# A product of constants behind every third piece of the chains between two attentions

## The chip, the core and the metric

The kernel runs on one core of a Trainium2 chip. The metric is the device time of one execution in microseconds (us). Five engines work beside each other and wait for one another by semaphores: PE (TensorE, matrix products; its weight loads are listed apart as PEld), DVE (VectorE), ACT (ScalarE), POOL (GpSimd) and SP (SyncE, which here only issues DMAs). Each engine takes its own instructions strictly in the order in which the program lists them; the profile also lists the clock that PE was granted, as a share of its full speed.

## The reference, cut to what matters

A stack of eight sublayers works on `x` of 8 batches x 512 tokens x 128 features, all in float32. Each one is `x = x + layernorm(f(layernorm(x)))`:

```
x = x + ln(L0_attn(ln(x)))   # softmax attention, 16 heads of 8
x = x + ln(L0_ffn (ln(x)))   # shifted mix, sigmoid(r) * (relu(k)^2 @ W_v)
x = x + ln(L1_attn(ln(x)))   # test-time learning: one gradient step after each batch
x = x + ln(L1_ffn (ln(x)))   # 8 experts, each token to its best one, capacity 256 an expert
x = x + ln(L2_attn(ln(x)))   # linear attention, softplus of normalised q and k
x = x + ln(L2_ffn (ln(x)))   # 8 experts, each takes its 512 best tokens
x = x + ln(L3_attn(ln(x)))   # softmax attention with rotary positions
x = x + ln(L3_ffn (ln(x)))   # 4 experts, each token weighs up to four of them
```

Nothing of this is touched by the change.

## The kernel before, in words

The 512 tokens of a batch lie as four tiles of 128. Three stretches follow one another. In the first, `Attention.run` works through the scores of L0's attention and a `Background` pulls pieces of the following sublayers in between. In the last, the same class does L3's attention with L3's expert layer in the background. Between the two lies the stretch that the change is about. There the sublayers from L0's feed-forward to the router of L2's experts are written as Python generators, here called chains: a chain issues the instructions of one piece of its work and yields.

- `residuals` (L556) finishes L0's attention batch by batch, `Mix.chain` (L616) is L0's feed-forward, `Learn.chain` and `serve_chain` (L760, L919) are the learning layer, `Route.chain` (L971) is the router of L1's experts, with its scatters to HBM at L1060.
- `Passes.chain` (L1107) runs L1's experts, in two passes (after 5 and after 8 routed batches); one piece is one expert: its input's transposes (L1136), hidden products (L1148, 128x256) and output products (L1170).
- `Pairs.chain` (L1234) sets off one `Pairs.batch` (L1252) every five turns. Such a chain of some 28 pieces takes one batch through the gather of L1's results (L1265), L2's linear attention (projection L1304, key-value sums L1335, outputs L1351) and L2's gate (L1392). The gradual start makes several batches lie side by side in different pieces.

`Rounds.turn` (L1202) sets the order: it lets every living chain issue one piece, in the order of its list, and is called until no chain is left. So the program order on every engine is chain after chain, turn after turn. A normalisation inside the chains goes DVE (statistics, L203), POOL (root, L194), DVE (offset, L211), ACT (scaling, L217), then PE (`flip`, four transposes, L239) and ACT (copy out of PSUM, L240).

Everything that PE writes goes to PSUM, by way of `Ctx.bank` (L118). It hands out the eight banks of PSUM in turn, whoever asks; whoever gets a bank waits until the readers of the bank's last content, eight requests ago, have finished.

`self.ident` and `self.c` are constants that lie in SBUF from the start: the identity, and behind it a triangular matrix and others.

Of the kernel before, what the change touches and what calls it, by code (L numbers as in the profile page):

```python
# [17 lines left out]
P = 128  # L18
# [10 lines left out]
C_ID = 0  # L29
# [41 lines left out]
class Ctx:  # L71


    def __init__(self, es: ExitStack, tc: tile.TileContext, consts: bass.AP):
        self.tc = tc
        nc = self.nc = tc.nc
        pool = lambda name, bufs, **kw: es.enter_context(tc.tile_pool(name=name, bufs=bufs, **kw))
        self.keep = pool("keep", 1)
        self.shared = pool("shared", 2)
        self.dram = pool("dram", 1, space=DRAM)  # L80

        self.c = self.keep.tile([P, C_ALL], F32, name="consts_sb", tag="consts_sb")
        nc.sync.dma_start(self.c, consts)
        self.ident = self.c[:, C_ID : C_ID + P]
        self.triu = self.c[:, C_TRIU : C_TRIU + P]
        self.ones = self.keep.tile([P, P], F32, name="ones", tag="ones")
        nc.vector.memset(self.ones, 1.0)
        self.mhalf = self.keep.tile([P, 8], F32, name="mhalf", tag="mhalf")
        nc.vector.memset(self.mhalf, -0.5)
        self.x = [self.keep.tile([P, NJ, D], F32, name=f"x{b}", tag=f"x{b}") for b in range(B)]  # L90

        self.home = self.keep

        self.ps = pool("ps", 1, space=PSUM)
        self.turn = [0]
        es.enter_context(tc.manual_schedule())

        self.brisk = False
# [19 lines left out]
    def bank(self, name):  # L118
        self.turn[0] += 1
        return self.ps.tile([P, 512], F32, name=name, tag=f"bank{self.turn[0] % self.RING}", bufs=1)  # L120

    def work(self, shape, name, bufs=2, dtype=F32):
        return self.w.tile(shape, dtype, name=name, tag=name, bufs=bufs)
# [137 lines left out]
class Background:  # L261
# [29 lines left out]
    def turn(self, gen):  # L291

        self.first.remove(gen)
        self.first.append(gen)
        self.step(self.first, gen)
# [897 lines left out]
class Rounds:  # L1193


    def __init__(self, chains):
        self.chains = list(chains)

    def add(self, chain):
        self.chains.append(chain)  # L1200

    def turn(self):  # L1202
        for chain in list(self.chains):
            try:
                next(chain)
            except StopIteration:
                self.chains.remove(chain)


class Pairs:  # L1210
# [520 lines left out]
def l3_weights(cx: Ctx, Wqkv, bqkv, Wout, bout):  # L1731
    raws = [cx.fetched(w) for w in (Wqkv, Wout)]
    rows = cx.row(bqkv, "w3a_b"), cx.row(bout, "w3a_bo")
    yield
    yield cx.transposed(Wqkv, "w3a", raw=raws[0]), cx.transposed(Wout, "w3a_o", raw=raws[1]), *rows
# [214 lines left out]
@with_exitstack  # L1950
def kernel(ctx: ExitStack, tc: tile.TileContext, a: dict, out: bass.AP):
    cx = Ctx(ctx, tc, a["consts"])
    nc = tc.nc
    for b in range(B):
        nc.sync.dma_start(cx.x[b], a["L0_attn_x"][b].rearrange("(j p) d -> p j d", p=P))
    of = lambda layer, *names: [a[f"{layer}_{n}"] for n in names]
    route = Route(cx, *of("L1_ffn", "w_switch", "b_switch"))
    right = ExitStack()
    with cx.phase("first"):
        cx.w = right.enter_context(tc.tile_pool(name="chains", bufs=2, side="right"))  # L1960
        with cx.beside("attention") as ca:
            mix = Mix(cx, *of("L0_ffn", "W_r", "W_k", "W_v", "mu_r", "mu_k"))
            learn = Learn(cx, route, *of("L1_attn", "t_k", "t_v", "t_q", "W1", "b1", "W2", "b2"))
            chains = l0(cx, Attention(ca), *of("L0_attn", "Wq", "Wk", "Wv"), mix, learn)

        cx.brisk = True
        with cx.beside("between") as cb:
            rounds = Rounds(chains)
            passes = Passes(cb, route, *of("L1_ffn", "w1", "b1", "w2", "b2"))
            pairs = Pairs(cb, route, *of("L2_attn", "W_qkv"), *of("L2_ffn", "gate_w"))  # L1970
            rounds.add(passes.chain())
            rounds.add(pairs.chain(passes, mix, rounds))
            while route.done < B:
                rounds.turn()
            right.close()
            ce = right.enter_context(cx.beside("experts", side="right"))
            experts = Experts(ce, pairs, *of("L2_ffn", "ln_w", "ln_b", "fc1s", "b1s", "fc2s", "b2s"))
            while rounds.chains:
                rounds.turn()
    cx.brisk = False  # L1980
    with cx.phase("last"):
        at = Attention(cx)
        ffn = L3Ffn(cx, *of("L3_ffn", "W1", "b1", "W2", "b2", "Wu", "bu"), out)
        with cx.beside("staging") as cs:
            cs.home = cx.home
            weights = l3_weights(cs, *of("L3_attn", "Wqkv", "bqkv", "Wout", "bout"))
            ffn.load()
            weights = experts.run(cs, weights)
        right.close()
        cx.w = right.enter_context(tc.tile_pool(name="tiles", bufs=2, side="right"))  # L1990
        with right:
            l3(cx, at, experts, ffn, weights)
# [62 lines left out]
```

## Time and profile before

| | |
|---|---|
| median of 3 runs | 2139.75 us (2133.82 to 2141.98) |
| the profiled execution's own time | 2144.43 us |
| its span, first to last instruction | 2142.6 us |
| granted PE clock, mean over the span | 0.876 |
| busy shares of the span | PE 83%, PEld 48%, DVE 59%, ACT 51%, POOL 23% |
| PE instructions (matmul records) | 10918 |
| shares of the chain that ended last | PE 59%, DVE 23%, issue 5%, POOL 5%, ACT 4%, DMA 2% |

The chain that ended last is followed back from the last instruction: at each step to what released it, or to the instruction before it on its engine. "Issue" is time in which an engine waited for nothing that the profile shows. The page cuts the span into 40 slices of 53.6 us. A float32 product is two matmul records and two weight loads, a transpose is one of each. The stretch between the attentions, from the end of the first attention's last products to the last pieces of `Pairs.batch`, goes from about 735 to 1125 us of the span.

### The profile page before, as it was taken

What the parts mean: (1) busy time and instruction counts of PE and PEld (TensorE: products, weight loads), DVE (VectorE), ACT (ScalarE), POOL (GpSimd) and SP (SyncE); (2) the same over time, 40 slices, a digit from 0 to 9 for tenths busy, and PEclk for the clock granted to TensorE, in tenths of its full rate; (3) what the DMA queues carried; (4) which work ended last, traced back from release to release, by engine and by line L of the source; (5) the groups of instructions that cost most, each with busy time, mean ns of one, the idle gap of its engine ahead of it and who ended that gap; (6) DMA issues with size and microseconds to landing.
All of it is one profiled execution on the core that took longest, in us unless ns stands there. A gap on an engine that the chain in (4) does not pass through costs nothing.

```text
span 2142.6 us, 31783 instructions
## 1 busy us (share of the span) xinstructions
PE 1772.7 (83%) x10918; PEld 1019.4 (48%) x10918; DVE 1265.6 (59%) x3840; ACT 1084.8 (51%) x2272; POOL 502.9 (23%) x574
## 2 busy tenths in 40 slices
PE   3999899999989757467646773899999999999998
PEld 1444445454444446446336552444444445454566
DVE  2677776868676455446547322776666666566322
ACT  1566655656545433246651221366666565656553
POOL 1001110212111130453523484222122121110010
PEclk7899999899889868579565786799999999999999
DMA  5212101111010103134323132111101011000000
GB/s 126 36 36 37 31 20 29 27 32 38 15 26 11 54 21 96 44 92 113 87 75 99 25 43 34 32 31 29 28 7 32 9 31 29 12 7 11 1 11 11
DMA packets 197920, 81.84 MB, mean 38 GB/s; under 512 B 97460, under 2 KB 189530, under 8 KB 197760
## 3 DMA queue, kind: packets, MB, share of 16 engines
q1 hardware_dynamic: 190080, 73.61, 14.3%
q0 software_dynamic: 7680, 6.19, 1.9%
q8 instruction: 88, 1.44, 0.3%
q14 instruction: 72, 0.59, 0.1%
HBM read 45.25 MB, written 31.59 MB: 36 GB/s over the span
## 4 chain that ended last, share of the span: by engine, by line
PE 59%; DVE 23%; issue 5%; POOL 5%; ACT 4%; DMA 2%; SPq 1%; POOLq 0%; ACTq 0%; DVEq 0%
PE at_s L402 13%; PE at_o L420 11%; DVE at_mx L403 8%; PE at_st L409 7%; PE l3f_y_ps L1923 5%; PE l3f_h_ps L1916 5%; DVE ln_st L203 3%; PE flip L239 3%; POOL l2f_out L1679 2%; POOL l2f_xg L1074 1%; POOL ln_rs L194 1%; PE l2a_qkv_ps L1304 1%; PE l1f_h_ps L1148 1%; PE l1f_y_ps L1170 1%; PE at_ops L434 1%
## 5 line engine op out<-in xcount | busy, mean ns | idle before, releaser
L403 DVE TENSOR_REDUCE at_mx<-at_s 128x1 f32<-128x512 f32 x1024 | 639.5, 681 | 281.4 <-PE at_st L409 217.8
L412 ACT ACTIVATE at_e<-at_st 128x512 f32<-128x512 f32 x1024 | 533.8, 597 | 214.0 <-PE at_st L409 189.3
L402 PE MATMUL at_s<-qk 32*128 32x512 f32 x2048 | 585.7, 652 | 28.1 <-DMA qk<-qk_zero 21.1
L409 PE MATMUL at_st<-qk 32*128 32x512 f32 x2048 | 567.3, 656 | 9.4 <-ACT at_e L412 4.6
L402 PEld LDWEIGHTS at_s<-qk 32*128 32x128 f32 x2048 | 221.4, 194 | 179.2 <-issue 74.0
L194 POOL TENSOR_TENSOR ln_rs<-ln_ve,mhalf 128x4 f32<-128x4 f32 x136 | 138.6, 1019 | 700.9 <-DVE ln_ve L188 607.3
L409 PEld LDWEIGHTS at_st<-qk 32*128 32x128 f32 x2048 | 218.4, 191 | 107.0 <-issue 41.5
L420 PE MATMUL at_o<-at_e,pad_v 128*32 128x512 f32 x2048 | 246.8, 625 | 9.9 <-DVE at_mx L403 9.8
L420 PEld LDWEIGHTS at_o<-at_e,pad_v 128*32 128x32 f32 x2048 | 63.5, 114 | 190.2 <-issue 156.9
L1923 PEld LDWEIGHTS l3f_y_ps<-w3f,l3f_hT 128*128 128x128 f32 x1024 | 129.3, 193 | 41.9 <-issue 30.9
L1923 PE MATMUL l3f_y_ps<-w3f,l3f_hT 128*128 128x128 f32 x1024 | 133.0, 277 | 0.6 <-ACT l3f_hT L1917 0.5
L1916 PE MATMUL l3f_h_ps<-l3f_xT,w3f 128*128 128x512 f32 x256 | 130.8, 606 | 0.1
L1917 ACT ACTIVATE l3f_hT<-l3f_h_ps,w3f_b1c 128x512 f32<-128x512 f32 x128 | 87.3, 689 | 84.0 <-PE l3f_h_ps L1916 83.8
L428 ACT COPY at_ot<-at_o 128x512 f32<-128x512 f32 x64 | 37.5, 586 | 173.8 <-PE at_o L420 173.8
L1926 DVE SCALAR_TENSOR_TENSOR l3f_o<-l3f_y_ps,l3f_w,l3f_o 128x128 f32<-128x128 f32 x128 | 44.5, 349 | 117.7 <-PE l3f_y_ps L1923 117.4
L217 ACT ACTIVATE l_xn<-x,ln_off,ln_rs 128x128 f32<-128x128 f32 x96 | 39.4, 482 | 72.4 <-DVE ln_off L211 72.3
L239 PE MATMUL flip<-consts_sb,l_xn 128*128 128x128 f32 x96 | 30.8, 411 | 47.8 <-ACT l_xn L217 47.6
L375 POOL COPY pad_v<-l_in 128x128 f32<-128x128 f32 x32 | 9.4, 293 | 246.2 <-DMA l_in<-l_v 216.0
L203 DVE BATCH_NORM_STATS2 ln_st<-x 128x6 f32<-128x128 f32 x256 | 55.2, 278 | 9.6 <-POOL x L1366 3.3
L1766 POOL TENSOR_TENSOR l_qk<-l_r,consts_sb 128x256 f32<-128x256 f32 x32 | 22.0, 687 | 159.0 <-DVE l_r L1761 159.0
L434 PE MATMUL at_ops<-consts_sb,at_ot 128*128 128x128 f32 x256 | 42.2, 288 | 18.1 <-DVE at_mx L403 16.6
L1679 POOL DMA_INDIRECT l2f_out<-l2f_y,l2f_idx x32 | 50.7, 1585 | 25.4 <-DVE l2f_y L1676 16.6
(388 smaller groups left out, 2514.7 us busy)
## 6 DMA issues: line engine op xcount, KB each, us to landing
l1f_w<-in_L_ffn_w SPq DMA_DIRECT2D x32, 256.0 KB
l2f_parts<-l2f_out SPq DMA_DIRECT2D x32, 256.0 KB
l2f_out<-l1f_zero SPq DMA_DIRECT2D x24, 256.0 KB
l_qk<-l_qkT SPq DMA_DIRECT2D x16, 256.0 KB
qk<-l_qk SPq DMA_DIRECT2D x128, 32.0 KB
qk<-at_mt SPq DMA_DIRECT2D x256, 2.0 KB
qk<-l_qkT SPq DMA_DIRECT2D x128, 32.0 KB
l2f_x<-l2f_rows SPq DMA_DIRECT2D x8, 272.0 KB
```

Of the source, the lines that this page charges most:

```text
L194: self.nc.gpsimd.tensor_tensor(rs, ve, self.mhalf[:, :NJ], ALU.pow)
L203: nc.vector.bn_stats(st[:, j, :], src[:, j, :])
L239: self.nc.tensor.transpose(t[:, j * P : (j + 1) * P], src[:, j, :], self.ident)
L402: nc.tensor.matmul(s, qk[:, 0, c * P : (c + 1) * P], qk[:, 1, :], start=True, stop=True)
L403: nc.vector.tensor_reduce(mx[n][:, c, h : h + 1], s, AX.X, ALU.max, negate=True)
L409: nc.tensor.matmul(s, qk[:, 1, c * P : (c + 1) * P], qk[:, 0, :], start=True, stop=True)
L412: nc.scalar.activation(es[g][:, h, :], s, AF.Exp, scale=scale)
L420: nc.tensor.matmul(o[32 * h : 32 * h + 32, :], vp[:, c, h, :], e[:, h, :], start=(c == 0), stop=(c == NJ - 1),)
L1679: nc.gpsimd.indirect_dma_start(out=self.pairs.summed[s], out_offset=bass.IndirectOffsetOnAxis(ap=idx[e][:, s : s + 1], axis=0), in_=ys[e][ ...
L1916: nc.tensor.matmul(hp, self.w1[:, e, f * P : (f + 1) * P], xt, start=True, stop=True)
L1917: nc.scalar.activation(hts[e][:, f], hp, AF.Relu, bias=self.b1c[:, f, e : e + 1])
L1923: nc.tensor.matmul(yp[:, :D], hts[e][:, f, js], self.w2[:, e, f, :], start=(f == 0), stop=(f == NF - 1))
```

## The change

`Ctx.stir` issues one product: the identity (128x128) with 256 columns of the constants, into the next bank of PSUM. Nothing reads it. `Rounds.turn` now calls it behind the third, the sixth and each further third chain of a turn's list. Nothing else is changed: with fewer than three living chains a turn issues no such product.

```diff
+    def stir(self):
+        self.nc.tensor.matmul(
+            self.bank("stir")[:, : 2 * P], self.ident, self.c[:, C_ID : C_ID + 2 * P], start=True, stop=True
+        )
...
 class Rounds:
-    def __init__(self, chains):
+    def __init__(self, cx: Ctx, chains):
+        self.cx = cx
         self.chains = list(chains)
...
     def turn(self):
-        for chain in list(self.chains):
+        for i, chain in enumerate(list(self.chains)):
             try:
                 next(chain)
             except StopIteration:
                 self.chains.remove(chain)
+            if i % 3 == 2:
+                self.cx.stir()
...
-            rounds = Rounds(chains)
+            rounds = Rounds(cx, chains)
```

## The prediction

> **What bounds the kernel now.** I began with the page's slices, to find the stretch of the change and PE's clock in it.
>
> ```profile
> PE   3999899999989757467646773899999999999998
> ...
> PEclk7899999899889868579565786799999999999999
> ```
>
> The stretch between the attentions is slices 13 to 20 (735 to 1125 us). PE is half to three quarters busy there and its granted clock falls to 0.5 to 0.8; both attentions stand at 0.9. Second, the busy times by stretch (PE, PEld, DVE, ACT, POOL, then clock, DMA share, GB/s):
>
> ```profile
> 735.00:800.00 65.00, 34.39 (x181) 28.88 (x178) 32.68 (x131) 17.39 (x40) 17.16 (x21) 0.63 0.17 51
> 800.00:828.00 28.00, 27.64 (x189) 24.70 (x187) 15.35 (x58) 13.09 (x31) 5.60 (x5) 1.00 0.42 118
> 828.00:950.00 122.00, 60.68 (x285) 49.03 (x286) 53.35 (x239) 34.84 (x80) 45.51 (x43) 0.65 0.18 51
> 950.00:997.00 47.00, 45.31 (x290) 40.07 (x289) 31.32 (x137) 30.04 (x66) 16.37 (x15) 0.97 0.54 158
> 997.00:1125.00 128.00, 69.85 (x236) 45.45 (x234) 67.36 (x364) 76.21 (x171) 51.34 (x48) 0.63 0.29 82
> ```
>
> Two kinds of stretch alternate. In 800 to 828 and 950 to 997, the two passes of L1's experts, PE is full and warm: 73.0 of 75 us. In the other 315 us no engine is full, PE is busy about half the time at a clock near 0.64, and the work hops from engine to engine. Third, the chain that ended last, cut to 735 to 1125: adding its pieces by engine gives PE 147 us, DVE 103, ACT 59, POOL 35, issue 26, DMA 18. Of PE's 147, 75 us lie where the granted clock was 0.5. What the clock is worth stands in the chain itself (start, duration, engine, tile, line, records):
>
> ```profile
> 771.35 3.47 PE l1a_a_ps L794 x16
> ...
> 805.90 1.73 PE l1f_h_ps L1148 x8
> ...
> 822.30 1.70 PE l1a_a_ps L794 x16
> ```
>
> The same sixteen records of L794 take 3.47 us at 0.5 and 1.70 at 1.0.
>
> Fourth, when the clock changes. [...]
>
> ```profile
> 788.95:792.36 3.41, 3.41 (x16) 3.14 (x15) 0.00 (x0) 1.82 (x3) 0.00 (x0) 0.50 0.02 5
> 826.50:829.91 3.41, 1.27 (x6) 0.77 (x5) 1.98 (x7) 0.95 (x2) 0.33 (x1) 1.00 0.64 182
> 853.80:857.22 3.42, 1.98 (x17) 1.90 (x17) 1.09 (x7) 0.15 (x1) 0.00 (x0) 1.00 0.36 117
> ...
> 1038.12:1041.54 3.42, 3.42 (x12) 2.20 (x12) 1.07 (x7) 2.80 (x8) 2.05 (x2) 0.50 0.72 197
> ...
> 1065.43:1068.84 3.41, 2.06 (x14) 1.53 (x13) 0.37 (x2) 2.37 (x5) 1.27 (x1) 1.00 0.01 2
> ```
>
> A cold slot filled with 128-column products (788.95) is followed by a warm one; a cold slot filled with transposes and 8-column products (1038.12) by a cold one. A warm slot 60% busy (1065.43) is followed by a warm one; at 58% (853.80) and 37% (826.50) the next is cold.
>
> Fifth, PE's timeline, to see what stands where the new products will stand:
>
> ```profile
> 952.85 1.89 PE L1148 MATMUL l1f_h_ps<-l1f_xT,l1f_w 128*128 128x256 f32 x8
> 954.58 1.45 PE L1304 MATMUL l2a_qkv_ps<-w2a,l_xT 128*128 128x384 f32 x4
> 955.87 0.38 PE L1136 MATMUL l1f_xT_ps<-consts_sb,l1f_xg 128*128 128x128 f32 x2
> ```
>
> Full stretches leave no gap at all. In a thin stretch it looks like this:
>
> ```profile
> 1013.89 1.25 PE L1351 MATMUL l2a_o_ps<-l2a_m,l2a_qT 128*128 128x144 f32 x8 [0.68 <-ACT l2a_qT L240]
> 1020.53 1.63 PE L239 MATMUL flip<-consts_sb,l_xn 128*128 128x128 f32 x4 [5.40 <-ACT l_xn L217]
> ```
>
> **The change part by part.**
>
> How many products. Walking the chains' yields gives 94 turns. The first 16 have six or seven chains and issue two each (32), the next 8 have five chains (8), the next 34 issue two in all but one (67), the next 26 have three to six chains and issue one, three of them two (29); the last ten issue none. Sum: 136, or 272 matmul records.
>
> What one costs. L1148 has its shape, 256 columns: eight records, four products, in 1.73 us at clock 1.0, so 0.43 us; at 0.5 twice that, 0.87, as with L794. Its weight loads I take as hidden, since L1148's are (PEld 0.19 us each beside it).
>
> Where they stand. PE's instructions stand in program order, so each product falls between two known matmuls. It starts when the earlier ends and pushes the later only by what exceeds the gap.
> - Full stretches: 31 products, 10 between 800 and 828 and 21 between 950 and 997, two of these before the clock rises. 29 x 0.43 + 2 x 0.87 = 14.2 us, of which the gaps take 0.3. Nothing hides them: PE is the bound and 96 to 99% busy. Cost 14 us.
> - The other 105 would take 73.6 us at the clock of their places. Gaps of PE, such as the 5.40 us before 1020.53, swallow 38.4; 35.2 us push PE's next matmul. At places where the chain that ended last runs through that matmul this is 16.1 us, all of it late. At the others, 19.1 us, the chain is on DVE, ACT, POOL or a DMA, and a later PE piece has slack. Bounds: 0 and 19.1; I take a third, 6.4, because PE holds about that share of the chain outside the full stretches. If that cover is gone, the 12.7 us more are paid too.
> - PSUM: each product takes a bank, so the ring comes round after five or six requests of the chains instead of eight. I compared the end of each bank's last reader with the moment its product would start: one wait, 0.45 us. No request of a chain gets a new wait either. Taken as 0.5; behind a waiting product all of PE's queue would stand.
> - DVE, ACT, POOL, SP and the DMA queues get nothing.
>
> What the clock gives back. A product streams 256 columns, more than the 128-column ones that warmed the slot after 788.95, so I count it as full work. Going through the slots with the products of each added, a cold slot reaches 90% of full work often, but the slot after it seldom stays above 60%: the products run at once behind earlier work, in a clump, and leave the late part of a gap as idle as it was. Chain pieces in slots that become warm: some 20 of the 75 us, which saves 10. Bounds: 0 (transposes and narrow products fill many of these slots, and 1038.12 says they don't count) and 75, which saves 37. The products that then run warm cost about 4 us less.
>
> Sum: 14 + 16.1 + 6.4 + 0.5 - 10 - 4 = +23 us; I take 21, since a push that lands in a wait for DVE or a scatter is lost again in the next turns. On the profiled execution's 2144.4 that is 2165; that execution lay 4.7 us over the median, so I predict 2139.75 + 21 = 2161. About 0.5%, 11 us, is what measurements of this kernel can tell from no change.
>
> [...]
> [...]
>
> **The rivals.**
>
> *One, faster: the clock holds.* Place: the thin stretches. If all 75 us of cold chain ran warm, 37 are saved, and the pushes outside the full stretches halve to 11: 14 + 11 + 0.5 - 37 = -12, 2128. For it: the products are dense work, and thin stretches at 52% busy lie not far under the 60% that held. Against: 853.80, which lost the clock at 58% busy. It decides from 56 us on: there 28 saved and 8 on cheaper pushes balance the 37 paid; below it the change costs.
>
> *Two, no change.* The off-chain pushes and half of the on-chain ones vanish in slack, and 30 us of chain become warm: 14 + 8 - 15 - 3 = +4, 2144. Against: the full stretches alone pay 14. Here too belongs that the product, read by nobody, is left out when the program is made: then 2140. I give that 2 in 100.
>
> *Three, worse.* All pushes are late and no slot warms: 14 + 35 = +49, 2189. For it: 1038.12, wholly busy, did not warm the next slot. With waits on banks it would be more still: L1148's bank has two readers of 0.47 us, and in the full stretches a product behind them could wait that long.
>
> **How the numbers follow.** My forecast, +11 to +36, has 0.52. Rival three takes 0.12, rival two 0.22, rival one 0.14. Slower by over 0.5%: 0.52 + 0.12 = 0.64; within: 0.22; faster: 0.14. The range goes from rival one's 2128 to the bound of rival three, 2188, leaving out 1 in 10 on either side.
>
> **What would show it.** PE should have 11190 matmul records. The expert passes should last 28 + 4 and 47 + 9 us with the clock still at 1.0; if they don't grow, the first term is wrong. Outside them the mean clock should rise from 0.64 to between 0.70 and 0.78; above 0.9 rival one is right, at 0.64 rival three. A PE wait released by ACT or DVE at a product's own line would show the bank ring. The last attention should keep its length. A span of this stretch at or under 390 us would refute the forecast.

## The result and the profile after

The changed kernel takes 2157.57 us (median of 10 runs, 2148.68 to 2168.27) against 2140.94 us (10 runs): ratio 1.0079, interval 1.0060 to 1.0099, so 16.6 us or 0.8% slower. The forecast was 21 us slower. A second measurement (experiment five) gave 1.0113, interval 1.0078 to 1.0149, or 24 us, so the two lie on either side of the forecast. The profiled execution has a span of 2152.1 us against before's 2142.6.

In the page of the kernel after, PE's row and its clock in the slices:

```profile
PE   3999899999989767679756773899999999999998
...
PEclk7899999899899788779775786799999999999999
```

Counted from 0, slices 13 to 20 have clock 7 to 9 where they had 5 to 9, and PE is busy 5 to 9 tenths where it was 4 to 7. The same page has the new products as one group (line, engine, operation, tiles, form, count, then busy us, mean ns of one, idle before):

```profile
L124 PE MATMUL stir<-consts_sb 128*128 128x256 f32 x272 | 94.8, 468 | 0.0
```

272 records are the 136 products that were counted, 11190 records in all, and PE never sat idle in front of one: in this profile no product waited for a bank. Busy times by stretch, bounds moved with the work:

```profile
735.00:800.00 65.00, 44.76 (x217) 35.96 (x216) 32.45 (x131) 16.10 (x38) 17.05 (x21) 0.76 0.17 51
800.00:832.00 32.00, 30.05 (x203) 27.22 (x201) 16.57 (x61) 13.31 (x30) 5.60 (x5) 1.00 0.41 117
832.00:950.00 118.00, 78.18 (x363) 62.23 (x363) 51.74 (x234) 34.75 (x79) 45.50 (x43) 0.75 0.16 44
950.00:1000.00 50.00, 47.30 (x281) 41.86 (x282) 28.82 (x125) 27.04 (x60) 15.56 (x15) 0.91 0.53 153
1000.00:1140.00 140.00, 90.25 (x366) 64.92 (x364) 76.32 (x379) 79.83 (x178) 57.76 (x61) 0.74 0.30 84
```

The thin stretches now have clock 0.74 to 0.76, up from about 0.64. The chain that ended last shows both sides of the account. In it PE's pieces of work at clock 0.5 shrank from 75.1 to 52.5 us, and 32.0 us of products are new (16.3 at full clock, 15.7 at half). PE's timeline shows where these stand:

```profile
960.44 0.59 PE L124 MATMUL stir<-consts_sb 128*128 128x256 f32 x2
960.87 1.45 PE L1313 MATMUL l2a_qkv_ps<-w2a,l_xT 128*128 128x384 f32 x4
962.16 0.59 PE L124 MATMUL stir<-consts_sb 128*128 128x256 f32 x2
962.59 0.38 PE L1142 MATMUL l1f_xT_ps<-consts_sb,l1f_xg 128*128 128x128 f32 x2
...
1025.37 0.59 PE L124 MATMUL stir<-consts_sb 128*128 128x256 f32 x2
1030.92 1.63 PE L245 MATMUL flip<-consts_sb,l_xn 128*128 128x128 f32 x4 [4.96 <-ACT l_xn L223]
```

In the pass each of these two begins 0.43 us before the work behind it. At 1025.37 one runs at the beginning of a gap, 4.96 us remain idle behind it, and the flip that ends the gap runs cold: four transposes in 1.63 us, as long as before.

For the experiments I measure the stretch between the attentions from the end of the last `at_ops` transpose to the end of the last `l2f_log_ps` product, since whole runs scatter by some 20 us from one to the next. This is the row of before, then the one of after, for that stretch:

```profile
736.60:1121.50 384.90, 236.30 (x1166) 187.18 (x1164) 198.93 (x920) 170.74 (x385) 135.98 (x132) 0.71 0.27 78
```

```profile
733.00:1130.30 397.30, 291.86 (x1438) 233.74 (x1436) 199.83 (x920) 171.83 (x385) 135.83 (x132) 0.80 0.26 76
```

384.9 against 397.3 us, so +12.4; in the second profile of the changed kernel 400.9, so +16.0. Each kernel below has one such profile, so a difference of some 4 us between two of them says little. "Cold time" below is the time in this stretch at clock 0.5: 227 us before, 161 and 168 in the two profiles after. A "slot" is 3.41 us, as in the rows of before: in this stretch each record of the clock, before and after, lasts 3.41 us or a multiple of it, at 0.5 or 1.0.

### The profile page after: what moved, and what is told of

It reads as the page before. It is cut to its first block, busy times and chain, and to the rows that moved or that the text cites. A ratio compares the mean times of both kernels' runs of the same rounds, so it can differ in the third digit from the quotient of the medians.

```text
span 2152.1 us, 32345 instructions
## 1 busy us (share of the span) xinstructions
PE 1826.4 (85%) x11190; PEld 1065.9 (50%) x11190; DVE 1266.2 (59%) x3840; ACT 1085.9 (50%) x2272; POOL 502.8 (23%) x574
## 4 chain that ended last, share of the span: by engine, by line
PE 60%; DVE 23%; issue 5%; POOL 4%; ACT 4%; DMA 2%; SPq 1%; POOLq 0%; ACTq 0%; DVEq 0%
PE at_s L408 12%; PE at_o L426 11%; DVE at_mx L409 8%; PE at_st L415 7%; PE l3f_y_ps L1932 5%; PE l3f_h_ps L1925 5%; PE flip L245 3%; DVE ln_st L209 3%; POOL l2f_out L1688 2%; PE stir L124 1%; PE l1f_h_ps L1154 1%; PE l1f_y_ps L1176 1%; PE l2a_qkv_ps L1313 1%; DVE ln_mv L211 1%; POOL l2f_xg L1080 1%
## 5 line engine op out<-in xcount | busy, mean ns | idle before, releaser
L124 PE MATMUL stir<-consts_sb 128*128 128x256 f32 x272 | 94.8, 468 | 0.0
L124 PEld LDWEIGHTS stir<-consts_sb 128*128 128x128 f32 x272 | 58.8, 238 | 11.3 <-issue 2.3
```

Of the source, the lines that this page charges most:

```text
L124: self.nc.tensor.matmul(self.bank("stir")[:, : 2 * P], self.ident, self.c[:, C_ID : C_ID + 2 * P], start=True, stop=True)
```

## The experiments

All ten were timed in five rounds against the kernel before on the same chip. Ratios are to it, with their 95% intervals.

**One and two: the products of the thin stretches alone, and those of the passes alone.** A flag is set while an expert pass issues its pieces:

```diff
-            if i % 3 == 2:
+            if i % 3 == 2 and not self.cx.dense[0]:    # one
+            if i % 3 == 2 and self.cx.dense[0]:        # two
```

> The products are issued only in turns in which no expert pass is running: 103 of 136 stay, the 33 of the two passes' pieces go. Theory (pushes less clock): in the passes PE is full and already warm, so the 33 products cost their own length there, 14 us, and bring nothing; without them the changed kernel's +16.6 us shrinks to about +3 (0 to +8, ratio 1.000 to 1.004), and the chain that ended last still holds some 20 us of products. Rival (the cost lies in the thin stretches, the passes have slack): still +12 or more.

> The products are issued only while an expert pass runs: 33 of 136. Theory: +14 us over the kernel before (+11 to +17, ratio 1.005 to 1.008), the passes longer by that and the thin stretches as before. Rival (the passes have slack): +5 or less.

One: ratio 1.0031 (1.0010 to 1.0052), stretch 393.0 us (+8.1), cold time 180 us. Two: 1.0038 (1.0014 to 1.0062), stretch 395.3 us (+10.4), cold time 234 us. The three rows of two are the stretch and the two passes, from the first `l1f_xT_ps` to the last `l1f_y_ps` of each:

```profile
740.70:1136.00 395.30, 251.24 (x1232) 199.52 (x1230) 199.86 (x920) 171.41 (x385) 136.04 (x132) 0.70 0.27 76
804.10:867.50 63.40, 50.70 (x334) 45.79 (x332) 32.27 (x108) 18.90 (x43) 6.63 (x6) 0.90 0.30 86
956.30:1008.60 52.30, 52.14 (x323) 46.59 (x323) 31.58 (x136) 30.67 (x66) 16.38 (x15) 0.96 0.50 146
```

The passes took 61.0 and 47.0 us before. So the 33 products cost 2.4 and 5.3 us there, and 2.7 us elsewhere. Products in the passes do cost, as the theory says, but 10 us and not 14.

Twelve of the 33 stand inside the first pass and 18 inside the second. In the trace of two each of them holds PE for 0.43 to 0.54 us until the next product or transpose begins (0.85 at half clock), 8.3 us in the second pass. That is the length that the forecast took. But the pass was not as full as its 96% says. These are the waits of PE's weight loads for the copies of the hidden layer in the second pass, before and then in two, and the longest of them in PE's timeline of before:

```profile
PEld l1f_y_ps L1170 <- DVE l1f_hT L1161: 2.0, 3, 1.6
PEld l1f_y_ps L1170 <- ACT l1f_hT L1159: 0.8, 1, 0.8
...
PEld l1f_y_ps L1177 <- DVE l1f_hT L1168: 0.4, 1, 0.4
```

```profile
972.08 1.83 PE L1170 MATMUL l1f_y_ps<-l1f_w,l1f_hT 128*128 128x128 f32 x14 [1.46 <-DVE l1f_hT L1161]
```

These waits fell from 2.8 to 0.4 us. That accounts for 2.4 of the 3.0 us by which the products' 8.3 us exceed the 5.3 that the pass grew. In the first pass the seventh input comes 2.8 us later than before, counted from the pass's start, and 2.7 of these are there at the fifth. Behind it one slot more runs at full clock, and the pass's cold time falls from 17.1 to 13.2 us, so its 2.4 us are not the price of the products alone: in the second profile of the changed kernel the pass had 17.1 us of cold time and took 65.6, 4.6 more than before.

The thin stretches cost 8.1 us net in experiment one, close to the forecast's reckoning for them (22.5 paid, 14 given back). The two parts don't add up to the whole in the stretches, 18.5 against 12.4 and 16.0. The ratios add up to 0.7%, against 0.8 and 1.1%, so the sum can't be tested closer than this scatter.

**Three: the banks without the products.** In place of the product one bank is passed over: `self.turn[0] += 1`.

> No product at all: where one stood, only one bank of PSUM is passed over, so the ring comes round as early as in the changed kernel. Theory: no bank has a reader that late, 0 us (ratio 0.998 to 1.002). Rival (part of the loss is PE waiting for banks that the products took from the ring): +5 us or more, with PE waits released by ACT or DVE copies out of PSUM.

Stretch 384.9 us, cold time 227 us: the same as before to 0.1 us. That the ring comes round earlier costs the chains nothing. It leaves open whether a product itself waits for its bank; in the second profile of the changed kernel one did, 0.90 us, among products that stand in a long gap of PE:

```profile
754.62 1.13 PE L124 MATMUL stir<-consts_sb 128*128 128x256 f32 x4 [0.90 <-DVE w1f_b L186]
```

The ratio is 0.9970 (0.9946 to 0.9993), though the stretch is unchanged; so a program can differ by 0.3% for reasons outside the stretch, and such a ratio alone decides nothing here.

**Four and six: transposes in place of the product,** two, then four:

```diff
+        for j in range(4):
+            at = slice(j * P, (j + 1) * P)
+            self.nc.tensor.transpose(t[:, at], self.c[:, C_ID + j * P : C_ID + (j + 1) * P], self.ident)
```

> In place of each product two 128x128 transposes of the same constants into the same bank: the same PE time (a transpose record of 128 columns takes as long as a product record of 256), the same bank. Theory: the transposes do not raise the clock, so the pushes are paid in full and nothing is given back: +30 to +45 us over the kernel before, mean clock of the stretch at or under the 0.70 of before. Rival (the clock matters little for the result, the pushes were simply smaller than summed): +17 us as with the products.

> Four 128x128 transposes in place of each product: two of them turned out to take half of a product's time (0.11 us a record in a row), so only four are the same PE time. Theory (transposes do not raise the clock): all pushes paid, nothing given back: the stretch 20 to 40 us longer than before's 385, its cold time at or over before's 227 us. Rival (the clock gives nothing back with the products either): as with the products, about 12 us longer.

Four: 1.0015 (0.9995 to 1.0035), stretch 392.1 us (+7.2), cold time 207 us. Its expectation was built on a wrong duration: in a row a transpose takes 0.11 us at full clock, so two are half a product. Six, with equal PE time: 1.0082 (1.0054 to 1.0110), stretch 403.1 us (+18.2), cold time 174 us. With the products the two profiles had 397.3 and 400.9 us, and 161 and 168 us of cold time, so this is their result within some 2 to 6 us. So the premise fell: with transposes the cold time went from 227 us to 207 and 174. One slot of experiment four shows it alone; all of PE's work in it is transposes, and the slot behind it is at full clock:

```profile
754.78:758.19 3.41, 3.41 (x17) 2.90 (x17) 3.04 (x20) 1.65 (x4) 2.56 (x3) 0.50 0.00 0
758.19:761.60 3.41, 0.86 (x6) 0.42 (x4) 2.18 (x7) 2.41 (x6) 3.06 (x3) 1.00 0.00 0
```

With that, six says nothing on what the clock gives back, and another experiment was needed: nine.

**Five: the changed kernel again,** on the chip of six to eight.

> The changed kernel itself, so that the others of this call can be held against it on the same chip. Ratio 1.006 to 1.010 to the kernel before, as in the first measurement; in the profile the stretch between the attentions some 12 us longer than before's 385.

1.0113 (1.0078 to 1.0149), stretch 400.9 us.

**Seven: two products at each place,** in one bank.

> Two products in a row at every place, into one bank. Theory: the passes pay twice (full stretches some +18 us), the thin stretches pay more pushes but run warm in most slots: the stretch 25 to 45 us longer than before, cold time under 100 us. Rival one (once the clock holds, the thin stretches gain more than they pay): stretch at most as long as with single products.

1.0199 (1.0163 to 1.0235), stretch 423.9 us (+39.0), cold time 126 us. The clock rises (0.85 over the stretch, against 0.80 and 0.79), and still each further product costs more than it brings: the chain that ended last now holds 76 us of products, against 29 and 32.

**Eight and ten: the products put where PE waits.** On the kernel before, `hold` issues a row of products just ahead of seven kinds of PE work that wait for another engine; the length of each row comes from the trace of before (the gap less 0.8 us, at 0.43 us a product). Ten lengthens the rows by what eight's trace left idle.

```diff
+    def hold(self):
+        n = next(self.plan[0], 0)
+        t = self.bank("stir") if n else None
+        for _ in range(n):
+            self.nc.tensor.matmul(t[:, : 2 * P], self.ident, self.c[:, C_ID : C_ID + 2 * P], start=True, stop=True)
...
     def flip(self, dst, src):
+        self.hold()
         t = self.bank("flip")
...
+            cx.plan[0] = iter(HOLD)   # eight: 0, 9, 0, 24, 1, ... 237 products; ten: 285
```

> The kernel before, with 237 products placed otherwise: none behind the chains, but in front of PE's waits of over 1.2 us (the first transposes of a normalised batch, the key-value sums, the router's products), as many as the wait in the trace of before holds at 0.43 us each, less 0.8 us. Theory: what decides is not the products' number but whether they fill the late part of a gap; with the gaps filled the clock holds (cold time of the stretch under 80 us against 227), the pushes stay small, and of the 75 us of cold chain 25 to 35 are saved: 10 to 30 us faster than before (ratio 0.986 to 0.995). Rival (pushes eat it up here too): ratio 1.000 or above.

> The held kernel with 285 products: where its trace left over 0.9 us of PE idle behind a row of products, the row is made longer by what fits. Theory (PE's cold pieces are worth little more, since the chain has gone over to DVE, ACT, POOL and DMAs): cold time falls from 89 to under 70 us, the stretch to 374 to 380 us, ratio to before 0.994 to 0.998. Rival (each cold microsecond on the chain still counts half): the stretch at 372 us or less, ratio under 0.993.

Eight: 0.9966 (0.9941 to 0.9992), stretch 379.5 us (-5.4), cold time 89 us. Ten: 0.9949 (0.9923 to 0.9975), stretch 375.3 us (-9.6), cold time 58 us. In the stretch both are shorter than both kernels; the whole run of ten lies at 2132.8 against 2144.4 us. Against the 0.3% that three showed without cause, eight's ratio is not enough by itself, and ten's is only 0.2% below three's. So the gain rests on the stretches, 5.4 and 9.6 us shorter where before and three agree to 0.1, and on their growing with the cold time that went. Eight's timeline shows a row:

```profile
739.64 10.63 PE L130 MATMUL stir<-consts_sb 128*128 128x256 f32 x48
752.05 1.64 PE L253 MATMUL flip<-consts_sb,l1f_xn 128*128 128x128 f32 x4 [1.78 <-ACT l1f_xn L230]
```

24 products fill the gap of 11.5 us in which the changed kernel ran six at once. Here 1.78 us were left, and the clock fell to half within the flip; ten gave that row three more, and there the flip stands wholly at full clock:

```profile
759.35 1.48 PE L253 MATMUL flip<-consts_sb,l1f_xn 128*128 128x128 f32 x4 [0.48 <-ACT l1f_xn L230]
```

So 1.7 and 2.1 times as many products as in the changed kernel leave a shorter stretch instead of a longer one: what differs is their places. The gain is less than expected for eight (10 to 30 us): cold pieces on the chain fell from 75.1 to 35.9 us, which at a half each would be 20 us, and the stretch fell by 5.4. In its place the chain holds 17.8 us of products. Nor is a piece at half clock always worth half: the four transposes of a flip at the end of a gap follow ACT's four pieces, which come 0.39 us apart. The eleven such flips of before that stand wholly at half clock take 1.63 or 1.64 us, the six of ten at full clock 1.48 or 1.49. Ten lies where its theory put it, with the stretch inside 374 to 380 us and the ratio inside 0.994 to 0.998, and not at the rival's 372 us or less.

**Nine: products of 8 columns, as long on PE.**

```diff
+        for j in range(2):
+            self.nc.tensor.matmul(t[:, j * 8 : j * 8 + 8], self.ident, self.c[:, C_ID : C_ID + 8], start=True, stop=True)
```

> In place of each product two products of 8 columns, four records: in a row such a record takes 0.105 us warm and 0.21 cold (eight of the gate's L1392 in 0.84 and 1.7 us), so PE is held for as long as by one product of 256 columns. In the trace of before, slots full of 8-column products stayed at clock 0.5. Theory (the clock that the products raise gives back some 10 us): without a raised clock the stretch is 22 to 32 us longer than before's 385 and its cold time at or over 210 us. Rival (the clock gives back next to nothing, the pushes alone make the 12 to 16 us): the stretch 12 to 16 us longer, with the clock as before.

1.0148 (1.0106 to 1.0189), stretch 416.4 us (+31.5), cold time 269 us. Two successive slots in it, both at half clock though the first has PE busy from end to end, 80% of it with these products:

```profile
753.68:757.09 3.41, 3.41 (x17) 3.06 (x16) 2.83 (x12) 2.07 (x6) 2.42 (x3) 0.50 0.00 0
757.09:760.50 3.41, 2.54 (x12) 2.45 (x12) 2.30 (x17) 1.52 (x4) 1.94 (x2) 0.50 0.01 2
```

For the same PE time the stretch is 15.5 to 19.1 us longer than with products of 256 columns. So the clock is worth something, and the rival, for which it is worth next to nothing, falls. How much the products give back against before's clock is not shown by this. Some of the difference is not a missing gain but a loss, since the cold time rose above before's 227 us: the first pass, 61.0 us before, took 72.4 here against 63.4 and 65.6 with the products, and 31.4 us of it were cold against 17.1 before.

## Why the prediction was right, and where its steps were off

- *The count, 136 products or 272 records:* exact.
- *Full stretches, +14 us:* the right sign and too large. Measured alone 7.7 us in the passes, 10.4 us over the stretch. The product's length was right, 0.43 us. The mis-sized term is what the gaps take, put at 0.3 us because PE's rows showed 96 to 99% busy: in the second pass alone the weight loads' waits fell by 2.4 us, and the first pass could win a slot of full clock that the sum did not count. The forecast's growth of the passes, 4 and 9 us, was 2.4 and 6.4 with all products in place, 4.6 and 6.0 in the second profile, where that slot stayed cold.
- *Thin stretches, 16.1 + 6.4 paid, 14 given back:* +8.5 in the sum, +8.1 us in the stretch of experiment one, ratio 1.0031. No run measures what was paid and what was given back apart, so part of the agreement may be luck. The forecast's 20 us of chain work that become warm were 22.6. The give-back itself stays open; nine only sets 15.5 to 19.1 us between the changed kernel and one whose clock fell.
- *The banks, 0.5 us:* no wait in one profile, one of 0.90 us in the other; for the chains 0.0 in experiment three.
- *The sum:* +23 us, taken as 21. The stretch, which the sum is about, grew by 12.4 and 16.0 us; that the whole run's 16.6 and 24 us lie on both sides of 21 is partly luck.
- *The clock, 0.64 to between 0.70 and 0.78:* 0.74 to 0.76 in the thin stretches.
- *Why the rows hold or lose the clock:* mostly wrong. I read the slot 1038.12, full of transposes and 8-column products, as saying that neither counts. With transposes the cold time fell from 227 us to 207 and 174 (four, six); with 8-column products it rose to 269 (nine). Nor did a warm slot need 60% of PE's busy time here. A slot of before that is 57% busy is followed by a warm one, and a slot of nine that is busy from end to end, half of it with 8-column products, by a cold one:

```profile
969.85:973.27 3.42, 1.96 (x16) 1.70 (x15) 3.38 (x20) 0.98 (x3) 1.96 (x2) 1.00 0.14 41
973.27:976.68 3.41, 3.41 (x25) 3.20 (x24) 1.96 (x11) 2.37 (x6) 2.18 (x3) 1.00 0.84 217
```

```profile
890.21:893.62 3.41, 3.41 (x31) 3.29 (x31) 2.20 (x11) 0.00 (x0) 1.28 (x2) 1.00 0.02 5
893.62:897.04 3.42, 0.38 (x3) 0.28 (x2) 2.38 (x10) 1.65 (x4) 2.86 (x3) 0.50 0.08 19
```

The columns of the records fit these slots better than busy time. Give each record, transpose or product alike, 0.84 ns a column (1.73 us for the eight records of 256 at 805.90), and twice that at half clock, and take the sum's share of the slot: 0.48 and 0.30 in the two slots above. In this stretch of before and of after together, the 85 warm slots with a warm one behind them have shares of 0.35 to 0.99, the 30 with a cold one 0 to 0.36; PE is busy for 45 to 100% of the former and for 0 to 88% of the latter. The 28 cold slots with a warm one behind them have shares of 0.75 and more, the 85 with a cold one 0 to 0.88. A line at 60% of busy time puts 12 of the 115 warm slots on the wrong side. Why the shares lie so no run shows. The 60% and the 90% by which the sum looked for slots that become warm were my estimate from five rows of before, and no run shows either; that its 20 us came near 22.6 is luck. With the gaps filled up to their end, 89 and 58 us of the stretch were cold (eight, ten); with products that often only begin a gap, 161 and 168.

- *The last attention keeps its length:* 815.8 us from its first projection before, 819.2 after; among the twelve profiles, all with the same code there, it ranges from 813.8 to 819.3, so that is scatter.

Rival one, the clock holds, needs 56 of the 75 cold microseconds. The products of the change reached 22.6; the held kernels reached 39.2 (35.9 left) and 45.3 (29.8 left). They are faster nevertheless; that their products, standing in gaps, pay fewer pushes is the likely reason, though pushes were not measured apart. Seven shows that more of the same products does not lead there.

## What to carry to other kernels

Work that is put in only to keep PE's clock up has to stand at the end of PE's gaps (285 products there made the stretch 9.6 us shorter), not behind the work in front of them (136 made it 12.4 and 16.0 us longer): PE ran the product at 1025.37 at the beginning of a gap, and the 4.96 us behind it stayed empty. Sum the places from the trace: what fits into gaps costs little (of eight's 237 products 17.8 us stand in the chain), and what stands in a full stretch is paid, less the waits that hide inside rows shown as busy (8.3 us of products made the second pass 5.3 us longer, since 2.4 us of waits went), so look at the weight loads' waits too. For the clock here, look at columns beside busy time: both slots above, 57 and 100% busy, went the other way than 60% says. And do not book half of every cold PE piece on the chain as gain: where 39 us of them went, the stretch became 5 us shorter, since other engines and the products themselves took their place in the chain, and transposes that wait for another engine piece by piece gain 0.15 of 1.63 us.

## What the runs showed that was not expected

Four transposes in place of one product left 174 us of cold time, the products 161 and 168, against 227 before. With products of 8 columns PE, busy through whole slots, stayed at 0.5, and cold time rose from 227 to 269 us. In the full second pass 18 products of 8.3 us in all lengthened it by 5.3 us, since 2.4 us of its weight loads' waits went. Slots of 3.41 us kept full clock with PE 57% busy and lost it with PE busy throughout.
